# A two-layer graph network with sorted row look-ups on one core: where a group's bias add and count comparison stand, and how many steps the woven streams are counted at

## The chip, the core and the metric

The kernel runs on one core of a Trainium2 chip. A core has a matrix engine (PE, with its weight loads shown as PEld), three engines for elementwise work (VectorE = DVE, ScalarE = ACT, GpSimd = POOL), a queue processor that issues most transfers (SyncE = SP), and 16 DMA engines. Each engine works through its own instruction queue in order and waits on semaphores for the others. The metric is the device time of one execution in microseconds, lower is better; the time of a kernel is the median of its runs.

## What is computed

Inputs are `x` (32 batches of 512 nodes with 256 features) and `adj` (32 x 512 x 512, zeros and ones). Two layers follow one another, each a graph operator and then a feed-forward block, with layer norms and residual sums. The change is in the first layer; its two parts, cut to what matters:

```python
def _L0_gnn_ref(x, adj, W_msg, W_upd, bias):
    a = adj.astype(x.dtype)
    h = jnp.einsum('bnf,fu->bnu', x, W_msg)
    msg_sum = jnp.einsum('bij,biu->bju', a, h)
    deg = jnp.sum(a, axis=1)
    messages = jnp.where(deg[..., None] > 0, msg_sum / jnp.maximum(deg, 1.0)[..., None], 0.0)
    return jax.nn.relu(jnp.einsum('bnf,fu->bnu', x, W_upd) + messages + bias)

def _L0_ffn_ref(x, Wt, bt, sl_cvx, of_cvx, sl_ccv, of_ccv, alpha, Wc, bc, Wg, bg, Wd, bd):
    s = jax.nn.sigmoid(alpha)
    t = jnp.max(xx[:, None, :] + Wt[None, :, :], axis=-1) + bt
    z = t[:, :, None]
    cvx = jnp.max(z * sl_cvx[None] + of_cvx[None], axis=-1)
    ccv = jnp.min(z * sl_ccv[None] + of_ccv[None], axis=-1)
    trop = s * cvx + (1.0 - s) * ccv
    classical = jax.nn.gelu(xf @ Wc + bc, approximate=False)
    g = jax.nn.sigmoid(xf @ Wg + bg)
    return (g * trop + (1.0 - g) * classical) @ Wd + bd
```

The second layer (graph attention with a softmax over typed edges, then a mixer over slices) is built by code that the change does not touch.

## The kernel before

**The maximum by look-ups.** `t` is, for each row of x, a maximum over 256 features of "value of the feature + that feature's row of the table `Wt`". The kernel does not form all 256 sums. For a row it takes the largest values in order, gathers the table rows that belong to them (a table in DRAM, 256 rows of 1024), and keeps a running maximum; after as many look-ups as are needed, smaller values cannot win. How many a row needs is counted for each row ahead of time (the column COUNT of its stored row). Rows are then sorted by that count, so that one tile of 128 rows holds rows of like need. `CAPS` gives the number of look-ups of the 32 tiles of a segment: 24, 9, 7, 6, 5, 5, 5, five times 4, four times 3, seven times 2, nine times 1. A flag `over` records for each row whether its count is above its tile's cap.

**Segments, tiles, groups.** The 32 batches make 4 segments of 8 batches (32 tiles of 128 rows). The feed-forward works on groups of 4 tiles: group g of a segment has the tiles g, g + 8, g + 16, g + 24, so g = 0 holds the tile with 24 look-ups ("heavy") and the others have few ("light"). The order of the 32 groups is (0,7), (0,0) to (0,6), (1,0) to (1,7) and so on.

**Three streams.** All are Python generators; every `yield` ends a step.

- `convs(s)`, one batch after the other: `conv_in` loads x and adj, normalizes (`layer_norm_T`: xna L56, its transposes lnpa L60, copies x1T L62) and multiplies by W_msg (ph L395, copied to h L397); `conv_out` multiplies by W_upd (pu L413, bias sum u L416), sums messages (pm L422, deg and u L425 to L427), normalizes the result (xnb L444), finds the eight largest values and their places (L448, L449), counts (rest L452), and stores the rows (`rows_of`, L458). `put_in_order` sorts a segment's rows.
- `features(raw)`, once at the start: it rearranges the feed-forward's features. A loop of six rounds (L283 to L303) of vector operations turns the slopes and offsets into bends; a key for each feature is stored and read back by all partitions (L328, L330); eight passes (L335) count how many keys are larger, one per block of 128 features; eight scatters (L339) put the features in order in DRAM; from there they are loaded (L348 to L350, L368), transposed (`turn`, L360, L361) and the table is stored (L365).
- `feed_forwards`: for each group `sums`, `mixed` and `down`.
  - `sums(s, g)` gathers the rows of the four tiles (xs L541), asks for the table rows of their largest value (best L552) and goes through the tiles: normalized rows xn (ACT, L562), their transposes into two PSUM tiles xsp (PE, L565), the bias of the output added to the residual in xs (POOL, L566), for caps above 8 more of the largest values (DVE), the comparison for `over` (DVE, L580), the value added to the first table row (ACT, L583), and then for each further look-up a gather of rows (POOL, L586) and a running maximum (DVE, L589, 128 x 1024). It yields after every fourth look-up and after every tile. At the end two copies turn xsp into xnT (ACT, L596).
  - `mixed(s, g)` goes through eight feature blocks f: cls and gate matmuls (PE, L609; ACT, L611), four transposes tz of the maxima (PE, L616), bends (ACT L618, L622; DVE L623), the mixture (DVE, L625 to L627). One step is one f, after a first one.
  - `down(s, g)` multiplies by W_d (po, L638), adds to the residual in xs (DVE, L640) and stores (L641).

**What sets the order.** `woven(a, na, b, nb)` (L68) takes steps of two streams in proportion na to nb. In the first phase convolutions of segment 0 run woven with `features` at 80 to 56. Later `feed_forwards` is woven with the rest of the convolutions and then with layer 1, which follows them. Within a group, `mixed` of the group is woven with `sums` of the next one at 9 to 8. That is the order of recording; a list scheduler of the tile framework then sets the order of each engine's queue by priorities and readiness, and inserts the semaphores. Tile pools bound how far the streams may overlap: a tile whose buffer is still read waits. Those that matter here: PSUM tags with two buffers each, "tp" (the two xsp of `sums`, the pair of a layer norm in `convs`, the transposes in `features`), "mm" (ph, pu, pm, po) and "mf" (cls, gate); in SBUF `best` with seven buffers (four to a group), `rows` with four, `xs` with three, `past` with three.

Of the kernel before, what the change touches and what calls it, by code (L numbers as in the profile page):

```python
# [10 lines left out]
BF16 = mybir.dt.bfloat16  # L11
U32 = mybir.dt.uint32
AF = mybir.ActivationFunctionType
ALU = mybir.AluOpType
# [4 lines left out]
P = 128  # L19
N = 512  # L20
D = 256
NT = N // P
# [74 lines left out]
def layer0_sorted(tc, ident, eps, x, adj, w, x2s, ranks, over, following):  # L97
# [6 lines left out]
    nc = tc.nc  # L104
    B = x.shape[0]
    SEG = B // len(x2s)
    ST = SEG * NT
# [3 lines left out]
    CAPS = [24, 9, 7, 6, 5, 5, 5] + 5 * [4] + 4 * [3] + 7 * [2] + 9 * [1]  # L111
# [3 lines left out]
    NG = ST // NT  # L115

    MEAN, COUNT, VAL, IDX, RW = D, D + 2, D + 3, D + 11, D + 19
# [9 lines left out]
    with ExitStack() as ctx:  # L127
        cst = ctx.enter_context(tc.tile_pool(name="c0", bufs=1))
# [24 lines left out]
        ones = cst.tile([P, 1], BF16, tag="ones0", name="ones0")  # L153
        nc.gpsimd.memset(ones, 1.0)

        count_to = cst.tile([P, P], I32, tag="count_to", name="count_to")
        nc.gpsimd.iota(count_to, pattern=[[1, P]], base=0, channel_multiplier=0)
        upto = cst.tile([P, P], BF16, tag="upto", name="upto")
# [49 lines left out]
        def features(raw):  # L208
# [52 lines left out]
            def pick(key, best):  # L261

                got = []
                for v in (sl, of):
                    other = part("other", four)
                    nc.vector.tensor_tensor(other, key, each(best), ALU.not_equal)
                    key = part("key", four)
                    nc.vector.scalar_tensor_tensor(key, other, -1e30, v, ALU.mult, ALU.add)
                    best = part("got", [P, FC, 2], bufs=4)
                    nc.vector.tensor_reduce(best, key, AX.X, ALU.max)  # L270
                    got.append(best)
                return got
# [11 lines left out]
            for s in range(NS + 1):  # L284
                d, t, out = part("d", four), part("t", four), part("out", four)
                nc.vector.tensor_sub(d, sl, each(slope))
                nc.vector.tensor_sub(t, of, each(offset))
                nc.vector.tensor_scalar(out, d, 0.0, None, ALU.is_le)
                nc.vector.tensor_scalar_max(d, d, 1e-30)
                nc.vector.reciprocal(d, d)  # L290
                nc.vector.tensor_mul(t, t, d)

                nc.vector.scalar_tensor_tensor(t, out, -1e30, t, ALU.mult, ALU.add)
                at = part("at", [P, FC, 2])
                nc.vector.tensor_reduce(at, t, AX.X, ALU.max)
                hit = hits[:, :, s, :]
                nc.vector.tensor_scalar(hit, at, -HI, None, ALU.is_gt)
                if s:
                    nc.vector.tensor_mul(hit, hit, hits[:, :, s - 1, :])
                steeper, offset = pick(t, at)  # L300
                nc.vector.tensor_sub(bend[:, :, s, :, 0], steeper, slope)
                nc.vector.tensor_copy(bend[:, :, s, :, 1], at)
                slope = steeper  # L303
                yield
# [28 lines left out]
            for c in range(FC):  # L333
                more = rtile("more", [P, FFN])
                nc.vector.tensor_scalar(more, every, place[:, 1, c : c + 1], 0.0, ALU.is_gt, ALU.add,  # L335
                                        accum_out=place[:, 2, c : c + 1])
            nc.vector.tensor_copy(number, place[:, 2, :])
            for c in range(FC):
                nc.gpsimd.indirect_dma_start(  # L339
# [191 lines left out]
        def feed_forwards():  # L531


            def sums(s, g):

                tiles = range(g, ST, NG)
                while s not in placed_segs:
                    next(ahead)
                xg = sb.tile([P, NT, RW], F32, tag="xs", name=f"xs{s}_{g}", bufs=3)
                for t, tile_no in enumerate(tiles):  # L540
                    nc.gpsimd.indirect_dma_start(  # L541
                        out=xg[:, t, :], out_offset=None, in_=rows_of[s],
                        in_offset=bass.IndirectOffsetOnAxis(
                            ap=order[:, s * ST + tile_no : s * ST + tile_no + 1].bitcast(U32), axis=0))
                xnT = sb.tile([P, DC, N], F32, tag="xnT", name=f"xnT{s}_{g}")
                pt = [ps.tile([P, NT, P], F32, tag="tp", name=f"xsp{s}_{g}_{c}") for c in range(DC)]
                best = []

                def ask(t):

                    best.append(sb.tile([P, FFN], F32, tag="best", name=f"best{s}_{g}_{t}", bufs=2 * NT - 1))
                    nc.gpsimd.indirect_dma_start(  # L552
                        out=best[t], out_offset=None, in_=table,
                        in_offset=bass.IndirectOffsetOnAxis(ap=xg[:, t, IDX : IDX + 1].bitcast(U32), axis=0))

                ask(0)
                for t, tile_no in enumerate(tiles):
                    if t + 1 < NT - 1:
                        ask(t + 1)
                    r, cap = xg[:, t, :], CAPS[tile_no]  # L560
                    xn = sb.tile([P, D], F32, tag="xn", name=f"xn{s}_{g}_{t}", bufs=2)
                    nc.scalar.activation(xn, r[:, :D], AF.Identity, bias=r[:, MEAN : MEAN + 1],  # L562
                                         scale=r[:, MEAN + 1 : MEAN + 2])
                    for c in range(DC):
                        nc.tensor.transpose(pt[c][:, t, :], xn[:, c * P : (c + 1) * P], ident)  # L565
                    nc.gpsimd.tensor_add(r[:, :D], r[:, :D], bd)  # L566
                    vals, idxs = r[:, VAL : VAL + 8], r[:, IDX : IDX + 8]
                    if cap > 8:
                        rounds = -(-cap // 8)
                        tops = sb.tile([P, 2, 8 * rounds], F32, tag=f"tops{rounds}", name=f"tops{s}_{g}_{t}", bufs=1)  # L570
                        vals, idxs = tops[:, 0, :], tops[:, 1, :]
                        for i in range(rounds):
                            eight = slice(8 * i, 8 * i + 8)
                            nc.vector.max(vals[:, eight], xn)
                            nc.vector.max_index(idxs[:, eight].bitcast(U32), vals[:, eight], xn)
                            if i + 1 < rounds:
                                less = sb.tile([P, D], F32, tag="xn", name=f"less{s}_{g}_{t}_{i}", bufs=2)
                                nc.vector.match_replace(less, vals[:, eight], xn, -3e38)
                                xn = less
                    nc.vector.tensor_scalar(over[:, s * ST + tile_no : s * ST + tile_no + 1],  # L580
                                            r[:, COUNT : COUNT + 1], 2.0 * cap + 1.0 - D, None, ALU.is_gt)
                    m = best[t]
                    nc.scalar.activation(m, m, AF.Identity, bias=vals[:, 0:1])  # L583
                    for k in range(1, cap):
                        row = sb.tile([P, FFN], F32, tag="rows", name=f"rows{s}_{g}_{t}_{k}", bufs=4)
                        nc.gpsimd.indirect_dma_start(  # L586
                            out=row, out_offset=None, in_=table,
                            in_offset=bass.IndirectOffsetOnAxis(ap=idxs[:, k : k + 1].bitcast(U32), axis=0))
                        nc.vector.scalar_tensor_tensor(m, row, vals[:, k : k + 1], m, ALU.add, ALU.max)  # L589
                        if k % 4 == 3:  # L590
                            yield
                    if t == NT - 2:
                        ask(NT - 1)
                    yield
                for c in range(DC):
                    nc.scalar.copy(xnT[:, c, :], pt[c].rearrange("p t n -> p (t n)"))  # L596
                got[s, g] = xg, xnT, best

            def mixed(s, g):
# [45 lines left out]
            groups = [(0, NG - 1)]  # L645
            groups += [(s, g) for s in range(len(x2s)) for g in range(NG) if (s, g) != groups[0]]
            yield from sums(*groups[0])
            for i, now in enumerate(groups):
                steps_ = mixed(*now)
                next(steps_)  # L650
                if i:
                    down(*groups[i - 1])
                yield
                more = sums(*groups[i + 1]) if i + 1 < len(groups) else iter(())
                yield from woven(steps_, 9, more, 8)
            down(*groups[-1])

        def all_convs():
# [10 lines left out]
        with tc.tile_pool(name="r0", bufs=1) as raw:  # L669
            first = iter(lambda: next(ahead), 0)  # L670
            next(first)
            bounds(raw)
            for _ in woven(first, SEG * 10, features(raw), 56):
                pass
        sb = ctx.enter_context(tc.tile_pool(name="s0", bufs=2, reuse_waits="tile"))

# [1547 lines left out]
```

## Time and profile before

| what | value |
|---|---|
| median of 3 runs | 4619.16 us (4616.48 to 4621.86) |
| the profiled execution, its own time | 4623.49 us |
| its span | 4621.6 us |
| mean granted PE clock | 0.951 |
| PE busy | 4067.9 us, 88% |
| DVE, ACT, POOL busy | 73%, 50%, 37% |
| first cls matmul of the feed-forward | at 324 us |
| last batch's rows of the convolutions stored | at 1906 us |
| layer 1 alone | from about 2500 us |

In the profile times are microseconds from the start of the span; Lnnn is a line of the kernel before. A line of the waits reads: engine, tile and line that waited, the engine, tile and line that ended the wait, total, times, longest. A line of the timeline reads: start, duration, engine, line, operation, tile written <- tiles read, shapes, number, and in brackets how long the engine was idle before it and what released it. In the rows of the costliest groups the number before the bar is a count, then busy time and mean nanoseconds of one, then the idle time ahead of it. Some matmul records are missing from the trace, so counts of matmuls in a short stretch can be too low.

### The profile page before, as it was taken

How to read it: one execution, taken by the hardware profiler on the slowest of the kernel's cores; microseconds unless marked ns; L12 is line 12 of the kernel's file. 1: busy time of each engine (PE TensorE's matmuls, PEld its weight loads, DVE VectorE, ACT ScalarE, POOL GpSimd, SP SyncE). 2: the span in 40 equal slices, each digit the busy share in tenths (PEclk: the TensorE clock that was granted, in tenths of full speed). 3: DMA queues.
4: the chain of work that ended last, by engine and by line, in shares of the span. 5: the costliest groups of instructions: out<-in, count | busy, mean ns of one | idle time of the engine just before them, and what ended most of it. 6: DMA issues, size and time to landing. Idle time of an engine off the chain costs nothing. (4 is left out here: it accounts for less than half of the span.)

```text
span 4621.6 us, 56127 instructions
## 1 busy us (share of the span) xinstructions
PE 4067.9 (88%) x19287; PEld 2525.4 (55%) x19287; DVE 3379.1 (73%) x7040; ACT 2291.7 (50%) x4756; POOL 1729.5 (37%) x2027
## 2 busy tenths in 40 slices
PE   5768898988988889888897899999999999999987
PEld 4545655656556566555554355555555555555555
DVE  6678778887788877777775777777787777777763
ACT  2344555545655556555564444545544454454432
POOL 2356444653435534353332223222323323332220
PEclk8889999999999999998998999999999999999998
DMA  5556433653436533374431111111111111111100
GB/s 125 172 158 214 164 127 126 198 178 124 136 118 198 177 129 112 99 263 145 141 115 48 53 46 56 51 48 44 44 54 49 56 56 53 47 54 56 40 14 15
DMA packets 235100, 474.09 MB, mean 103 GB/s; under 512 B 38299, under 2 KB 114075, under 8 KB 234804
## 3 DMA queue, kind: packets, MB, share of 16 engines
q0 software_dynamic: 80256, 282.38, 19.3%
q1 hardware_dynamic: 154548, 188.02, 13.3%
q8 instruction: 154, 2.52, 0.2%
q14 instruction: 142, 1.16, 0.1%
HBM read 413.16 MB, written 57.16 MB: 102 GB/s over the span
## 5 line engine op out<-in xcount | busy, mean ns | idle before, releaser
L609 PE MATMUL clsp<-xnT,wc 128*128 128x512 f32 x1024 | 512.1, 621 | 77.3 <-ACT cls L611 63.0
L609 PE MATMUL gatep<-xnT,wg 128*128 128x512 f32 x1024 | 497.7, 605 | 16.0 <-ACT gate L611 13.2
L638 PE MATMUL po<-wd,acc 128*128 128x256 f32 x2048 | 450.9, 381 | 0.4 <-DVE acc L627 0.3
L638 PEld LDWEIGHTS po<-wd,acc 128*128 128x128 f32 x2048 | 391.4, 191 | 65.9 <-issue 13.8
L422 PE MATMUL pm<-h,adj 128*128 128x257 f32 x1024 | 295.5, 435 | 136.3 <-DVE xs L640 67.3
L589 DVE SCALAR_TENSOR_TENSOR best<-rows,xs,best 128x1024 f32<-128x1024 f32 x212 | 276.1, 1305 | 165.4 <-ACT best L583 98.1
L623 DVE SCALAR_TENSOR_TENSOR acc<-past,fld,acc 128x512 f32<-128x512 f32 x448 | 351.1, 787 | 54.3 <-ACT past L622 45.5
L1198 DVE SCALAR_TENSOR_TENSOR att<-own,other,mask 128x512 f32<-128x512 f32 x512 | 378.9, 762 | 11.5 <-DMA own<-ownd 11.0
L586 POOL DMA_INDIRECT rows<-table,xs x212 | 261.1, 1232 | 237.3 <-DVE best L589 171.8
L609 PEld LDWEIGHTS gatep<-xnT,wg 128*128 128x128 f32 x1024 | 195.8, 195 | 260.5 <-issue 197.0
L622 ACT ACTIVATE past<-tz,fld 128x512 f32<-128x512 f32 x448 | 291.0, 694 | 83.4 <-DVE acc L623 83.0
L618 ACT ACTIVATE acc<-tz,fld 128x512 f32<-128x512 f32 x256 | 199.5, 779 | 265.1 <-PE tz L616 262.0
L422 PEld LDWEIGHTS pm<-h,adj 128*128 128x128 f32 x1024 | 212.4, 218 | 194.5 <-issue 106.7
L1231 PE MATMUL avp<-att,hv 128*64 128x512 f32 x1024 | 310.3, 628 | 4.2 <-DVE att L1198 4.2
L609 PEld LDWEIGHTS clsp<-xnT,wc 128*128 128x128 f32 x1024 | 185.7, 197 | 222.3 <-issue 121.1
L1331 PE MATMUL yTp<-sw,x 128*128 128x512 f32 x512 | 242.7, 614 | 39.8 <-DVE sw L1326 32.3
L611 ACT ACTIVATE cls<-clsp,fld 128x512 f32<-128x512 f32 x256 | 176.7, 690 | 201.7 <-PE clsp L609 86.9
L1319 PE MATMUL lgp<-wsl,x4T 128*128 128x512 f32 x512 | 252.0, 628 | 27.9 <-DVE mask L1070 21.7
L1139 POOL DMA_INDIRECT x<-x2s,ranks x128 | 140.9, 1101 | 343.0 <-DVE att L1198 104.1
L1284 POOL TENSOR_TENSOR mu<-mu,eps 128x16 f32<-128x16 f32 x32 | 121.3, 3791 | 324.2 <-DVE mu L1283 323.1
L611 ACT ACTIVATE gate<-gatep,fld 128x512 f32<-128x512 f32 x256 | 175.6, 686 | 127.5 <-PE gatep L609 103.6
L541 POOL DMA_INDIRECT xs<-rows_of,order x128 | 143.4, 1121 | 250.7 <-DVE acc L623 78.7
(597 smaller groups left out, 8961.5 us busy)
## 6 DMA issues: line engine op xcount, KB each, us to landing
adji<-in_adj SPq DMA_DIRECT2D x128, 256.0 KB
ai<-in_adj SPq DMA_DIRECT2D x128, 256.0 KB
own<-ownd SPq DMA_DIRECT2D x128, 256.0 KB
rows_of<-keep SPq DMA_DIRECT2D x32, 550.0 KB
x<-in_x SPq DMA_DIRECT2D x32, 512.0 KB
x2s<-xs SPq DMA_DIRECT2D x32, 512.0 KB
out<-x SPq DMA_DIRECT2D x32, 512.0 KB
rows<-table,xs POOLq DMA_INDIRECT x212
```

The lines of the kernel that those rows point to most:

```text
L422: nc.tensor.matmul(pm[:, : D + 1], a[:, i, t * P : (t + 1) * P], h[:, i, :], start=i == 0, stop=i == NT - 1)
L586: nc.gpsimd.indirect_dma_start(out=row, out_offset=None, in_=table, in_offset=bass.IndirectOffsetOnAxis(ap=idxs[:, k : k + 1].bitcast(U32) ...
L589: nc.vector.scalar_tensor_tensor(m, row, vals[:, k : k + 1], m, ALU.add, ALU.max)
L609: nc.tensor.matmul(pf, wf[:, c, f * P : (f + 1) * P], xnT[:, c, :], start=c == 0, stop=c == DC - 1)
L611: nc.scalar.activation(o, pf, fn, bias=fld[:, f, bf : bf + 1], scale=1.0 if fn == AF.Gelu else 0.5)
L622: nc.scalar.activation(r, z, AF.Relu, bias=fld[:, f, AT + b : AT + b + 1])
L623: nc.vector.scalar_tensor_tensor(y, r, fld[:, f, CH + b : CH + b + 1], y, ALU.mult, ALU.add)
L638: nc.tensor.matmul(po[:, i, :], acc[f][:, t * P : (t + 1) * P], wd[:, f, :], start=f == 0, stop=f == FC - 1)
L1198: nc.vector.scalar_tensor_tensor(e, own[h], other[:, j, h : h + 1], mask[:, j, :], ALU.max, ALU.mult)
L1231: nc.tensor.matmul(pv[q][k * HO : (k + 1) * HO, :], hv[:, j, h, :HO], weighed[b, h, j], start=j == 0, stop=j == NT - 1)
L1319: nc.tensor.matmul(pf, xnT[:, c, t * P : (t + 1) * P], wsl[:, c, :], start=c == 0, stop=c == DC - 1)
L1331: nc.tensor.matmul(py, xn[:, t, c * P : (c + 1) * P], sw[:, t, :], start=t == 0, stop=t == NT - 1)
```

## The change

It has three parts.

1. In `features`, three places yield more: two in each of the six rounds and one after each of the eight counting passes (20 more steps); the count at which `features` is woven goes from 56 to 74.
2. In `sums`, the bias add and the comparison leave the loop over tiles and stand at the end of the group: one comparison over the four tiles against a constant tile `limits` of 128 x 32, which nine memsets on POOL fill at the start, and four bias adds.
3. `mixed` and the next `sums` are woven at 9 to the number of steps that these sums have, one for each tile and one for each four look-ups: 11 for g = 0, then 7, 6, 6, 5, 5, 5, 5 for g = 1 to 7, in place of 8 always.

```diff
+        limits = cst.tile([P, ST], BF16, tag="limits", name="limits")
+        for i, cap in enumerate(CAPS):
+            if i == 0 or cap != CAPS[i - 1]:
+                nc.gpsimd.memset(limits[:, i:], 2.0 * cap + 1.0 - D)
...
                 nc.vector.tensor_scalar_max(d, d, 1e-30)
+                yield
                 nc.vector.reciprocal(d, d)
...
                     nc.vector.tensor_mul(hit, hit, hits[:, :, s - 1, :])
+                yield
                 steeper, offset = pick(t, at)
...
                 nc.vector.tensor_scalar(more, every, place[:, 1, c : c + 1], 0.0, ALU.is_gt, ALU.add,
                                         accum_out=place[:, 2, c : c + 1])
+                yield
...
-                    nc.gpsimd.tensor_add(r[:, :D], r[:, :D], bd)
...
-                    nc.vector.tensor_scalar(over[:, s * ST + tile_no : s * ST + tile_no + 1],
-                                            r[:, COUNT : COUNT + 1], 2.0 * cap + 1.0 - D, None, ALU.is_gt)
...
                 for c in range(DC):
                     nc.scalar.copy(xnT[:, c, :], pt[c].rearrange("p t n -> p (t n)"))
+                nc.vector.tensor_tensor(over[:, s * ST : (s + 1) * ST].rearrange("p (t g) -> p g t", g=NG)[:, g, :],
+                                        xg[:, :, COUNT], limits.rearrange("p (t g) -> p g t", g=NG)[:, g, :],
+                                        ALU.is_gt)
+                for t in range(NT):
+                    nc.gpsimd.tensor_add(xg[:, t, :D], xg[:, t, :D], bd)
...
-                yield from woven(steps_, 9, more, 8)
+                steps = sum(1 + CAPS[n] // 4 for n in range(groups[(i + 1) % len(groups)][1], ST, NG))
+                yield from woven(steps_, 9, more, steps)
...
-            for _ in woven(first, SEG * 10, features(raw), 56):
+            for _ in woven(first, SEG * 10, features(raw), 74):
```

## The prediction

> **What bounds the kernel now.** First the page's busy times, then busy time by stretch: start of the layer, feed-forward with the next convolutions woven in, feed-forward alone, layer 1. Columns of the second: stretch, length, busy us (instructions) of PE, PEld, DVE, ACT, POOL, granted clock, DMA share, GB/s.
>
> ```profile
> PE 4067.9 (88%) x19287; PEld 2525.4 (55%) x19287; DVE 3379.1 (73%) x7040; ACT 2291.7 (50%) x4756; POOL 1729.5 (37%) x2027
> ...
> 0.00:324.00 324.00, 207.04 (x874) 161.93 (x875) 209.34 (x764) 111.87 (x238) 118.03 (x316) 0.84 0.50 147
> 324.00:2057.00 1733.00, 1523.45 (x5760) 1000.95 (x5759) 1355.75 (x2669) 943.56 (x1617) 862.46 (x1131) 0.96 0.49 157
> 2057.00:2500.00 443.00, 400.61 (x1419) 243.79 (x1418) 313.24 (x439) 254.19 (x402) 150.87 (x137) 0.95 0.38 122
> 2500.00:4621.00 2121.00, 1936.85 (x11240) 1118.74 (x11238) 1500.76 (x3171) 982.05 (x2501) 598.15 (x444) 0.97 0.16 47
> ```
>
> PE is the bound. Layer 1 (from 2500) keeps its order, so the change can only touch PE's idle time before it: 324 − 207 = 117 us, 1733 − 1523 = 210 us, 443 − 401 = 42 us. Next the waits of 324 to 2500 (total us, times, longest), to see what that idle time is:
>
> ```profile
> PE pm L422 <- DVE xs L640: 67.3, 16, 8.0
> PE clsp L609 <- ACT cls L611: 63.0, 41, 6.3
> ...
> PE ph L395 <- DVE xs L640: 16.0, 2, 8.6
> ```
>
> ```profile
> DVE best L589 <- ACT best L583: 110.7, 21, 7.4
> ...
> DVE over L580 <- DMA xs<-rows_of,order: 46.1, 45, 6.7
> ```
>
> ```profile
> POOL xs L566 <- ACT xn L562: 207.0, 51, 14.6
> ```
>
> The two named parts wait visibly: the comparison (L580) 46.1 us on DVE, the bias add (L566) 207.0 us on POOL. PE's largest waits, 67.3 + 16.0 = 83.3 us in 18 waits, are for the residual add (L640), at boundaries between groups. One of them in the timeline (start, duration, instruction, idle before it):
>
> ```profile
> 1054.34 0.60 PE L616 MATMUL tz<-ident,best 128*128 128x128 f32 x4
> ...
> 1056.06 1.03 POOL L552 DMA_INDIRECT best<-table,xs  x1 [0.16 <-issue]
> ...
> 1063.37 1.15 ACT L583 ACTIVATE best<-best,xs 128x1024 f32<-128x1024 f32 x1 [4.92 <-DMA best<-table,xs]
> ...
> 1066.16 5.25 DVE L589 SCALAR_TENSOR_TENSOR best<-rows,xs,best 128x1024 f32<-128x1024 f32 x4 [6.60 <-ACT best L583]
> ...
> 1081.24 0.68 DVE L640 TENSOR_TENSOR xs<-xs,po 128x512 f32<-128x512 f32 x1
> ...
> 1082.07 2.48 PE L422 MATMUL pm<-h,adj 128*128 128x257 f32 x5 [7.76 <-DVE xs L640]
> ```
>
> The chain: the last transpose (1054.34) frees `best`; its gather lands; ACT adds the value (1063.37); DVE's row maxima start (1066.16, 11.8 us after the transpose) and the second residual add stands behind them on DVE; PE waits 7.76 us. Steps or no steps, these sums cannot start before that transpose.
>
> **The change part by part.** All prices are against the profiled run, 4623.5 us (span 4621.6); the median shown is 4619.2, 4.3 lower. The built queues give the new order.
>
> *Comparison and bias.* DVE loses 128 comparisons of 147 ns and gains 32 wider ones, at about the old row's longest, 155 ns: 18.8 − 5.0 = 13.9 us of busy time, credited at 0 since DVE is 78% busy (1355.75/1733) where PE waits for chains. The scheduler does not leave the comparison at the end: in the built order it stands where the gathers land, one wait in place of four. It matters where an overdue comparison holds DVE, in the last groups, with no convolution beside them:
>
> ```profile
> 2319.82 0.15 DVE L580 TENSOR_SCALAR over<-xs 128x1 f32<-128x1 f32 x1 [1.39 <-DMA xs<-rows_of,order]
> ...
> 2320.66 0.69 ACT L611 ACTIVATE gate<-gatep,fld 128x512 f32<-128x512 f32 x1 [2.35 <-DVE acc L626]
> ...
> 2321.40 1.99 PE L609 MATMUL clsp<-xnT,wc 128*128 128x512 f32 x4 [2.29 <-ACT gate L611]
> ```
>
> Two comparisons waited 1.16 + 1.39 there, behind them stood the mixing's L626, for which ACT's gate waited, and PE lost 2.29 behind that. Five such groups at about half of it: −6. Bounds: −11.5 if all of it is gained; +6 if the one comparison waits for the fourth gather with L626 still behind it, as long again as half of the two did (2.55/2 × 5). The 128 adds of 747 ns stay on POOL, queued near their tile, so POOL's 207 us stay too; behind them stand gathers for the next tile, and only 8.2 us of PE waited on an add: 0 (±8).
>
> The nine memsets (98 ns each by L152: 0.9 us) lie in POOL's 8.85 us wait at 3 to 12 us: 0; without that cover, 0.9.
>
> [...]
>
> *Step counts.* 9 against 8 becomes 9 against 11 for sums of g = 0, then 7, 6, 6, 5, 5, 5, 5. Fewer steps mean that the next group's sums are recorded faster through the mixing. At seven light boundaries the built order holds the two "tp" buffers for the sums until the mixing ends, so that the convolution's layer norm comes later, into the boundary: 8 lnpa transposes (2 × 0.60) and 16 ph (3.78), 5.0 us of PE. The ACT work goes with it, ahead of the value adds: two xnT (0.59 each), xn 0.60, xna 0.59, four xnb (0.59), two x1T (0.59), four rest (0.51), two h (0.57): 9.1 us. ACT idled 4.92 at this place (the row at 1063.37), so 4.2 to 4.5 us stick out, and the row maxima start that much later; PE has 5.0 us more to do meanwhile. Net about −0.5 each, called 0. Bounds: all 9.1 us in the way, +4.1 × 7 = +29; none, −5.0 × 7 = −35.
>
> Before heavy mixings (g = 0; after groups 6 and 14) some 16 us of convolution matmuls now stand ahead of `po`, and there
>
> ```profile
> 852.04 3.78 PE L395 MATMUL ph<-w_msg,x1T 128*128 128x256 f32 x8 [7.44 <-DVE xs L640]
> ```
>
> had a twin of 8.57. Both waits go, −16.0; eight row maxima more stand in those gaps, 8 × 1.28 = 10.2, of which I take half as exposed: −11. Bounds −16 to +10 (waits stay, all eight exposed).
>
> *Features in shorter steps.* 20 more yields against 18 more in the count. Counted in steps, the chain ends at 73.5 of some 100 convolution steps (68 × 80/74; before 48 × 80/56 = 68.6): 4.9 steps, at 12 a batch of about 20 us, 8 us later. SP's queue says more: there the store of `keys`, the loads of `sorted_rows` and the store of `table` each stand behind one more batch's `rows_of`, so about 20 us later. The last copies of the chain run at 212 now; at 232 they still lie ahead of the first gather from `table` (275) and the first cls (324), so the cover, 275 − 212 = 63 us, holds; with it gone the delay would be paid in full, +8 to +20. Stage one's DVE work only changes places between batches. Five comparisons in a row, with 7.6 us of waiting at 268 to 276, stand ahead of a convolution's bias sum; one wait is left of them. I take −2 (−10 to +10, as batches before or after get the DVE first).
>
> SP's other changes are loads of x that pass a load of adj or a store of x2s at a few boundaries; SP waits for nothing new, and each issue took about 0.38 us (L379, L641): 0.
>
> Sum: −6 + 0 + 0 − 11 − 2 = −19, of which I take off 5 for new waits that such a reordering leaves elsewhere (PE's 63.0 us on cls L611 are the next in line): −14. 4623.5 − 14 = 4609.5; on the median's footing 4605.
>
> **Rivals.**
> *Slower: ACT in the way.* Place: the seven light boundaries, ACT's queue ahead of the value add L583. If most of the 9.1 us is new delay, each costs +4.1: +29, the heavy −11 fails too, −6 − 2 + 5 stay: about +26, 4645. It decides once the row maxima start 7.5 us or more later than 11.8 after the last transpose (2.5 × 7 = 18 cancels the gains). For it: PE waits 83 us at just these boundaries already. Against it: ACT's 4.92 us idle and 50% load.
>
> *Nothing.* The scheduler puts comparison and adds back where their data land, and the features' chain has its cover; the boundaries cancel: 4619 ± 5. For it: the built order does the first; against it, that nine boundaries do change.
>
> *Far faster.* The 5.0 us moved in costs no delay, as PE waits 7.76 there: −35 − 11 − 6 − 2 + 5 = −49, 4570. For it: ACT's idle time; against it: the row maxima wait for ACT (110.7 us).
>
> **How the numbers follow.** Forecast 0.42, ACT in the way 0.27, nothing 0.16, far faster 0.15. A measurement tells 0.2% (9.2 us) from no change. The forecast's own spread (4590 to 4617) is beyond that line three times in four; so faster 0.42 × 0.75 + 0.15 = 0.47, same 0.10 + 0.15 = 0.25, slower 0.28. The range 4572 to 4646 leaves out half of the far faster case and half of the slower one: 0.2.
>
> **What would show it.** Right: row maxima about 16 us after the last transpose at light boundaries, PE's wait for L640 down from 83 to about 65 us, the two heavy waits gone, comparisons' wait below 35 us, POOL's wait for xn still near 200, the features' last copies near 232 and the first cls still at 316 to 326, layer 1 as long as before (2121). Wrong: row maxima 19 us or more after it and L640's waits above 100 us; first cls past 330, which would mean that the features' chain or its convolutions lost their cover; or a new wait of over 20 us in the feed-forward that no row above names.

## The result, and the profile after

| | before | after |
|---|---|---|
| median of 8 runs | 4622.19 us (4607.51 to 4635.2) | 4602.43 us (4594.19 to 4612.24) |
| ratio to before | | 0.9967, 95% interval 0.9947 to 0.9986 |
| span of the profiled execution | 4621.6 us | 4610.5 us |
| first cls matmul | 324.0 | 327.0 |
| first matmul of layer 1 behind the feed-forward | 2514.6 | 2507.4 |

The change makes the kernel faster by 0.33% (0.14 to 0.53%), 15 us by the ratio; the prediction said 4605 us. The ratio, made of runs side by side on a chip, is what counts: the medians of before alone wandered between 4614 and 4622 from one set of runs to the next. The profiled execution after took 4612.2 us, 10 more than its kernel's median.

The same view by stretch as ahead of the prediction (stretch, length, busy us and instructions of PE, PEld, DVE, ACT, POOL, granted clock, DMA share, GB/s), for the kernel after:

```profile
0.00:324.00 324.00, 204.08 (x859) 158.99 (x860) 206.73 (x751) 109.53 (x234) 113.12 (x321) 0.85 0.50 147
324.00:2057.00 1733.00, 1545.08 (x5796) 1007.99 (x5794) 1356.65 (x2619) 948.52 (x1624) 880.13 (x1140) 0.95 0.49 158
2057.00:2500.00 443.00, 400.42 (x1418) 241.71 (x1416) 306.48 (x413) 252.32 (x399) 144.51 (x133) 0.95 0.37 118
2500.00:4611.00 2111.00, 1929.39 (x11218) 1110.23 (x11218) 1498.45 (x3163) 981.76 (x2501) 596.13 (x443) 0.97 0.16 47
```

In the second stretch PE is busy 21.6 us longer (1545.1 against 1523.5), that is, idle by as much less; the start is idle 3 us longer and the last groups of the feed-forward as long as before. Where the idle time went shows in PE's waits of 324 to 2500:

```profile
PE clsp L619 <- ACT cls L621: 56.4, 36, 7.4
PE pm L430 <- DVE xs L650: 40.4, 14, 6.0
PE pm L430 <- DVE u L435: 37.4, 12, 6.4
PE clsp L619 <- ACT gate L621: 18.7, 15, 5.9
...
PE ph L403 <- DVE xs L650: 8.7, 2, 4.4
```

and, of the kernel before, three that are needed here and below:

```profile
PE pm L422 <- DVE u L427: 20.2, 9, 6.2
...
PE lnpa L60 <- ACT xna L56: 8.3, 4, 5.3
PE pm L422 <- DVE u L416: 7.8, 6, 2.2
```

The residual add's waits (L640 before, L650 now) fell from 67.3 to 40.4, and those of ph from 16.0 to 8.7: from 83.3 to 49.1 us in all. Another wait rose: that of the message matmul pm for u (L427 before, L435 now), from 20.2 to 37.4. DVE and POOL, the two that the change names:

```profile
DVE over L602 <- DMA xs<-rows_of,order: 55.0, 16, 8.4
```

```profile
POOL xs L606 <- ACT xn L570: 189.6, 34, 17.9
```

A third of the waits, but not less waiting: 55.0 us in 16 against 46.1 in 45 for the comparison, 189.6 against 207.0 for the bias add.

The boundary between groups (1,1) and (1,2), the same one as ahead of the prediction, in the timeline of the kernel after:

```profile
1047.30 0.60 PE L626 MATMUL tz<-ident,best 128*128 128x128 f32 x4
...
1053.11 3.77 PE L403 MATMUL ph<-w_msg,x1T 128*128 128x256 f32 x16
...
1058.21 1.15 ACT L588 ACTIVATE best<-best,xs 128x1024 f32<-128x1024 f32 x1
...
1063.05 2.60 DVE L594 SCALAR_TENSOR_TENSOR best<-rows,xs,best 128x1024 f32<-128x1024 f32 x2 [4.58 <-ACT best L588]
...
1075.19 0.68 DVE L650 TENSOR_TENSOR xs<-xs,po 128x512 f32<-128x512 f32 x1
1075.82 1.28 DVE L594 SCALAR_TENSOR_TENSOR best<-rows,xs,best 128x1024 f32<-128x1024 f32 x1
...
1076.02 1.98 PE L430 MATMUL pm<-h,adj 128*128 128x257 f32 x8 [2.74 <-DVE xs L650]
...
1077.62 1.27 DVE L594 SCALAR_TENSOR_TENSOR best<-rows,xs,best 128x1024 f32<-128x1024 f32 x1
```

The last of DVE's row maxima in the kernel before, ahead of its second residual add at 1081.24:

```profile
1077.12 1.28 DVE L589 SCALAR_TENSOR_TENSOR best<-rows,xs,best 128x1024 f32<-128x1024 f32 x1 [0.41 <-DMA rows<-table,xs]
1078.77 2.54 DVE L589 SCALAR_TENSOR_TENSOR best<-rows,xs,best 128x1024 f32<-128x1024 f32 x2 [0.37 <-DMA rows<-table,xs]
```

The convolution's ph (3.77 us) stands in the boundary now, and lnpa beside it. The value add runs 10.9 us after the group's last transposes (1058.21 − 1047.30; before 9.0) and the row maxima start 15.7 us after them (before 11.8), 3.9 us later. But the second residual add comes only 1.0 us later than before (27.9 after the transposes against 26.9): two of the nine row maxima, at 1075.82 and 1077.62, now stand behind it, where all nine stood ahead, and 2 × 1.28 = 2.6 us is most of the difference. PE waits 2.74 us in place of 7.76. That is 5 us of work put into a wait that grew by 1.0.

The same matmuls stand in six boundaries now, after (0,1), (0,2), (1,0), (1,1), (2,0) and (2,1). PE's idle time from the last transposes to the message matmul that waits for the second residual add, summed from the timeline, was 7.8, 4.1, 7.6, 7.8, 7.8 and 8.0 us and is 3.2, 3.2, 5.0, 3.3, 3.6 and 3.3, 21.5 us less. The second of them is a check of the reading: after (0,2) no row maximum moved behind the second residual add, and there the add is as late as the row maxima (4.1 and 3.8 us later than before) and PE gains only 0.9 us.

### The profile page after: what moved, and what is told of

The parts are those of the page before. It is cut to its first block, busy times and chain, and to the rows that moved or that the text cites. A ratio compares the mean times of both kernels' runs of the same rounds, so it can differ in the third digit from the quotient of the medians.

```text
span 4610.5 us, 56109 instructions
## 1 busy us (share of the span) xinstructions
PE 4079.0 (88%) x19287; PEld 2518.9 (55%) x19287; DVE 3368.3 (73%) x6944; ACT 2292.1 (50%) x4756; POOL 1733.9 (38%) x2036
## 3 DMA queue, kind: packets, MB, share of 16 engines
q14 instruction: 141, 1.16, 0.1%
## 5 line engine op out<-in xcount | busy, mean ns | idle before, releaser
L619 PE MATMUL clsp<-xnT,wc 128*128 128x512 f32 x1024 | 526.6, 633 | 76.5 <-ACT cls L621 56.4
L591 POOL DMA_INDIRECT rows<-table,xs x212 | 253.0, 1193 | 215.7 <-DVE best L594 160.3
L619 PEld LDWEIGHTS clsp<-xnT,wc 128*128 128x128 f32 x1024 | 188.3, 201 | 226.4 <-issue 121.3
L621 ACT ACTIVATE cls<-clsp,fld 128x512 f32<-128x512 f32 x256 | 175.1, 684 | 208.6 <-PE clsp L619 102.3
L1342 PE MATMUL yTp<-sw,x 128*128 128x512 f32 x512 | 243.7, 617 | 36.4 <-DVE sw L1337 29.0
```

What stands on the lines that cost most here:

```text
L591: nc.gpsimd.indirect_dma_start(out=row, out_offset=None, in_=table, in_offset=bass.IndirectOffsetOnAxis(ap=idxs[:, k : k + 1].bitcast(U32) ...
L619: nc.tensor.matmul(pf, wf[:, c, f * P : (f + 1) * P], xnT[:, c, :], start=c == 0, stop=c == DC - 1)
L621: nc.scalar.activation(o, pf, fn, bias=fld[:, f, bf : bf + 1], scale=1.0 if fn == AF.Gelu else 0.5)
L1342: nc.tensor.matmul(py, xn[:, t, c * P : (c + 1) * P], sw[:, t, :], start=t == 0, stop=t == NT - 1)
```

## The experiments

All ratios are to the kernel before, from runs on the same chip, with their 95% intervals. "Stage" is the stretch from the first cls matmul to the first matmul of layer 1, and idle its length less PE's busy time, both from the view by stretch: 2190.6 − 1928.6 = 262.0 us before, 2180.4 − 1942.6 = 237.8 after.

**1. The step counts alone.**

```diff
-                yield from woven(steps_, 9, more, 8)
+                steps = sum(1 + CAPS[n] // 4 for n in range(groups[(i + 1) % len(groups)][1], ST, NG))
+                yield from woven(steps_, 9, more, steps)
```

> Before with nothing changed but the step count at which the next group's sums are woven (11 for g = 0, then 7, 6, 6, 5, 5, 5, 5 instead of 8). Theory (the order around the heavy mixings makes the gain): nearly the whole gain of the change is here, -10 to -20 us against before (ratio 0.996 to 0.998), PE's wait for the residual add (L640) in 324 to 2500 down from 83 to about 50 us, and the mixing of g = 7 with its heavy sums 10 to 25 us longer but that of g = 0 about 15 shorter. Rival (the comparison and bias at the end make it): within 4 us of before, L640's waits still near 83.

Measured: 4604.32 us, ratio 0.9971 (0.9961 to 0.9982), −13 us; stage idle 241.0; the residual add's waits 45.3 + 8.5 us. The gain of the change is here.

**2. Comparison and bias at the end, alone**: the parts of the change in `sums` with `limits`, 8 steps, features as before.

> Before with only the comparison and the bias adds at the end of a group's sums (and the nine memsets). Theory: within 5 us of before (ratio 0.999 to 1.001): DVE has some 10 us less to do but is not the bound, and the one comparison waits for the last of four gathers, so its waits are not below before's 46 us. Rival: -8 us or more, with L640's waits down by 30 us.

Measured: 4609.65 us, ratio 0.9977 (0.9966 to 0.9989), −11 us, more than the theory allows; stage idle 256.7 (5 less than before), first cls 3 us sooner (320.6), the comparison's wait 56.9 us in 18, the residual add's waits 54.1 + 16.0. Neither side has it: the rival's time, but not its mark (the waits down by 30 us; they fell by 13).

**3. The features' shorter steps alone**: the three yields and the count 74.

> Before with only the 20 more yields in the features' chain and the count 74. Theory: the first cls matmul, which came at 324 in before and at 327 in the change, comes at 324 to 330 and the time is within 5 us of before (ratio 0.9995 to 1.001): the cover of 63 us holds. Rival 1 (the shorter steps help the convolutions): first cls at 316 or sooner and -6 us. Rival 2 (the chain's cover is gone): first cls past 335 and +10 us.

Measured: 4620.92 us, ratio 1.0006 (0.9991 to 1.002), first cls at 325.9, stage idle 261.3. No gain, and nothing lost that this can tell; the first theory stands.

**4. The change without the features' part.**

> The changed kernel with the features' chain as before (no added yields, count 56). Theory: as the change or a few us faster, -12 to -20 us against before (ratio 0.9957 to 0.9975), first cls back at 324. Rival (the features' steps carry part of the gain): only -5 us or less.

Measured: 4607.35 us, ratio 0.9977 (0.9967 to 0.9988), −11 us; stage idle 243.7. Slightly less than forecast, but beside 0.9971 for the steps alone and 0.9967 for the whole the intervals overlap. What follows: the ends add nothing that shows on top of the steps, though alone they showed −11 us. It is not that both move the same convolution work into the boundaries: in the profile of run 2 ph still stands ahead of the last transposes after (1,1), and PE's idle time at that boundary is within half a microsecond of the kernel before. Why the ends help alone stays open.

**5. and 6. The step counts taken apart**: 11 for the heavy sums alone, and the light groups' counts alone.

```diff
-                yield from woven(steps_, 9, more, 8)
+                steps = 11 if groups[(i + 1) % len(groups)][1] == 0 else 8
+                yield from woven(steps_, 9, more, steps)
```

> Before with the step count 11 only where the next group is g = 0, else 8 as before. Steps alone gave -13.4 us (ratio 0.9971). Theory (both places share it): the pairs of groups around the heavy mixings of segments 0 to 2 lose 3 to 7 us each, none where the convolutions are done (group (3,0)), in all -5 to -10 us against before; PE's idle time within 20 us after a light boundary as in before (7.8 us at the boundaries after groups (0,1), (1,1), (2,1)). Forecast as it was made: -11. Rival (light boundaries make it all): within 3 us of before.

```diff
                 steps = sum(1 + CAPS[n] // 4 for n in range(groups[(i + 1) % len(groups)][1], ST, NG))
+                if groups[(i + 1) % len(groups)][1] == 0:
+                    steps = 8
                 yield from woven(steps_, 9, more, steps)
```

> Before with the step count of each light group's sums (7, 6, 6, 5, 5, 5, 5) and 8 as before for g = 0. Theory: PE's idle time after the boundaries behind (0,1), (1,1), (2,1) falls from 7.8 to about 3.3 us, as in steps alone, since 5 us of convolution matmuls lie there and the row maxima start only 1 to 2 us later; a part comes back as waits of the message matmuls for u (L427), 20 us in before; -4 to -9 us against before. The forecast had about 0 here. Rival (ACT in the way): +5 us or more, row maxima 16 us or more after the last transpose.

Measured: heavy 4609.18 us, ratio 0.9998 (0.9987 to 1.0008); light 4592.33 us, ratio 0.9961 (0.9948 to 0.9974). The rival of the first has it: the light groups make the whole gain, −18 us, twice what the theory of the second gave them, and the 11 steps nothing that the time shows. Stage idle was 253.8 in the heavy run and 241.6 in the light one. The wait of ph for the residual add, heavy and light:

```profile
PE ph L395 <- DVE xs L640: 15.0, 2, 7.7
```

```profile
PE ph L395 <- DVE xs L640: 9.0, 2, 4.7
```

It was 16.0 before: the light counts shorten it, the 11 steps hardly. The same boundary as above in the run with the light counts, in the timeline:

```profile
1033.21 3.77 PE L395 MATMUL ph<-w_msg,x1T 128*128 128x256 f32 x16
...
1056.51 2.90 PE L422 MATMUL pm<-h,adj 128*128 128x257 f32 x8 [3.13 <-DVE xs L640]
```

ph is in the boundary and PE's wait is 3.13 us; the idle time at the six boundaries is 22.5 us below that of the kernel before (3.5, 3.0, 3.4, 3.7, 3.5, 3.5). The row maxima are as late as in the change, 15.7 us after the last transposes at (1,1), close to the 16 or more that the rival had named; its loss is not there. PE's waits of 324 to 2500 by name:

```profile
PE clsp L609 <- ACT cls L611: 50.2, 34, 7.3
PE pm L422 <- DVE u L427: 39.6, 12, 6.2
PE pm L422 <- DVE xs L640: 34.8, 15, 4.6
```

The residual add's wait is lower still than in the change (34.8 against 40.4), and u is as high (39.6 against 20.2 before): some of the gain comes back one step later. That DVE, with row maxima still to do, is then late for the next message matmuls is the likely reason; no run takes it apart.

**7. The comparison in the last stage of the group**: the change, with the comparison taken out of `sums` and put into `down`, once a group, behind its two residual adds (not twice, as the expectation has it).

> The changed kernel with the comparison moved once more, from the end of the group's sums into the last stage of the group (after each residual add, so twice a group). Theory: DVE's 55 us of waiting for the gathers at the comparison goes to under 10, but DVE is not the bound there, so within 5 us of the changed kernel (ratio against before 0.996 to 0.998). Rival (the comparison's wait holds the mixing's DVE work and through ACT the PE): -8 us or more against the changed kernel, PE's wait of clsp for ACT (56 us) down by 15 us.

Measured: 4600.67 us, ratio 0.9972 (0.9963 to 0.9982): no different from the change. But its wait did not go: 55.7 us in 16, the same, and in the last groups it waits 2.7 to 2.8 us each time for the same gathers as in the change. The scheduler put the comparison back where its data land, so this run can't tell what that wait costs; that stays open.

**8. The down projection copied out of PSUM by ACT**, on top of the change.

```diff
-                    nc.vector.tensor_add(xg[:, t0 : t0 + 2, :D], xg[:, t0 : t0 + 2, :D], po)
+                    pc = sb.tile([P, N], F32, tag="past", name=f"poc{s}_{g}_{t0}", bufs=3).rearrange("p (t d) -> p t d", t=2)
+                    nc.scalar.copy(pc, po)
+                    nc.vector.tensor_add(xg[:, t0 : t0 + 2, :D], xg[:, t0 : t0 + 2, :D], pc)
```

> The changed kernel with the down projection copied out of PSUM by ACT, into a buffer of the bends (past), and the residual add reading the copy: ACT has 64 copies of about 0.6 us more, 38 us, and DVE's adds no longer hold the two mm buffers. Theory (what is left at the boundaries is that the second residual add stands behind the row maxima on DVE): PE's waits for the residual add, 40.4 + 8.7 us in the changed kernel, are gone, and the time falls by 15 to 35 us against it (ratio against before 0.989 to 0.994). Rival (the next thing, DVE's u, ends the wait at the same time): the same wait shows up as pm waiting for u, and the time is within 5 us of the changed kernel. Rival 2: the copies stand ahead of the value adds on ACT and cost 5 us or more.

Measured: 4570.04 us, ratio 0.9905 (0.989 to 0.992), −44 us against before and some 29 against the change; stage idle 225.4. No wait for the residual add is left, and the theory has the time. It doesn't have all of the account: stage idle fell by only 12.4 where 49.1 us of waits went, since cls (56.4 to 68.8), u (37.4 to 46.8) and lnpa (6.5 to 15.4) are waited for longer and ph waits 7.6 us for the copy. Part of what rival 1 named is there. The other 24.1 us by which this profile's stage is shorter are shorter matmuls; the last section comes back to these.

**9. and 10. The copy with the light counts, without and with the ends.**

> Before with the light groups' step counts (8 kept for g = 0) and the down projection copied out of PSUM by ACT; neither the features' steps nor the ends. Theory (the two gains lie at the same boundaries, but one fills PE's wait and the other removes it, so they overlap): light steps gave -18 us, the copy -30 us on top of the change; together -40 to -52 us against before (ratio 0.989 to 0.9915), and a few us faster than the changed kernel with the copy (0.9905) since the 11 steps of g = 0 cost 3 to 6 us a heavy group. Rival (the copy alone does it, the step counts then have nothing to fill): as the changed kernel with the copy or slower, 0.9905 to 0.993.

> As the run before (light steps, copy by ACT) with the comparison and bias at the end of the sums added. Theory (the ends only take some waits from DVE that is not the bound): within 5 us of it. Rival (the ends are worth the -10 us they showed alone): 8 us or more faster than it.

Measured: 4575.34 us, ratio 0.9907 (0.9891 to 0.9923), and 4569.67 us, ratio 0.9901 (0.9884 to 0.9917). Runs 8, 9 and 10 can't be told apart: the step for g = 0 and the ends make no difference that shows, as the theory of the second had it, and the few us that the theory of the first promised are not seen. Run 9's ratio lies within its rival's bounds too; that the copy alone does not do it is for run 12 to show. Any of the three is faster than both kernels; the last by 46 us against before.

**11. Five steps for every group, the heavy ones too.**

```diff
-                yield from woven(steps_, 9, more, 8)
+                yield from woven(steps_, 9, more, 5)
```

> Before with 5 in place of 8 for every group, the heavy ones too: that is what half of the light groups got, and 6 less than the change gives g = 0. Theory (what pays is that the next group's sums of a light group are recorded to their end inside the mixing; for heavy sums fewer steps leave more of the look-ups behind the mixing): -10 to -22 us against before (ratio 0.995 to 0.998), the three triples of groups around a heavy mixing as with light steps or up to 4 us longer. Rival (the heavy groups need their steps): each triple 6 us or more longer than in before and the whole within 3 us of it.

Measured: 4592.23 us, ratio 0.9957 (0.9942 to 0.9971), −20 us; stage idle 226.4. A constant does as well as the count by look-ups, and heavy sums with 5 steps lose nothing that the time shows: the number must be small for the light groups, and that is all that these runs show of it.

**12. The copy by ACT alone**, on the kernel before.

> Before with only the down projection copied out of PSUM by ACT; steps 8, no other part of the change. Theory (the change's gain is that convolution matmuls fill PE's wait for the residual add; take that wait away and there is nothing left to fill): PE's waits for the residual add, 83 us in before, are gone, and the time is near that of the copy with the step counts (0.9901 to 0.9907): -34 to -46 us against before (ratio 0.990 to 0.9927). Rival (the step counts pay by themselves): -15 to -30 us (ratio 0.9935 to 0.9967), so that the steps still add 14 us or more on top.

Measured: 4599.91 us, ratio 0.9965 (0.995 to 0.998), −16 us: the theory is wrong and the rival's time is met. PE's waits, 324 to 2500:

```profile
PE clsp L609 <- ACT cls L611: 94.2, 45, 8.8
PE pm L422 <- DVE u L427: 45.2, 12, 9.4
PE lnpa L60 <- ACT xna L56: 19.2, 7, 5.4
PE pm L422 <- DVE u L416: 15.7, 8, 3.1
```

The 83.3 us for the residual add are gone, as they should be, but clsp's wait rose by 31 (63.0 to 94.2), u's by 33 (20.2 + 7.8 to 45.2 + 15.7), lnpa's by 11: 75 of the 83 come back under other names, and stage idle fell by only 15.6 (to 246.4). Freed from one buffer, PE ran ahead and stopped at the next thing in its queue. With the light counts as well (run 9), which put convolution work there, stage idle is 227.9, and the two together give 0.9907, where apart they gave 0.9961 and 0.9965.

## Why the prediction was right, and where its sum was not

The time, the direction and the size are right (4605 forecast, 4602 measured), and what was said of the bound is right: what was gained is idle time of PE before layer 1. The terms of the sum are not right: errors of both signs cancel, so that the total came out as forecast is luck.

- *Light boundaries, "Net about −0.5 each, called 0"*: wrong. Run 6 gives −18 us (−12 to −24). The 5.0 us of PE work did move in, and the row maxima do start 3.9 us later at (1,1), where 4.2 to 4.5 were forecast and "about 16 us after the last transpose" was the mark (15.7). The step that failed is the next one: that delay was carried over whole to the second residual add, which PE waits for, as if everything ahead of it on DVE stayed ahead of it (as it does after (0,2) alone). In the new queue two row maxima of 1.28 us have moved behind it there and after (2,1), one at three of the other places, and it came 1.0 us later. So some 5.0 − 1.0 = 4.0 is gained at such a place (21.5 over the six, 3.6 each), near what the rival "far faster" took (5.0); that rival's total was too high, as the heavy part and the last groups gave nothing that shows and the wait of pm for u rose. PE's waits for the residual add fell to 49.1, where 65 was the mark.
- *Heavy mixings, "−11"*: wrong. Run 5 gives −1 us (−6 to +4), though its stage idle is 8 us lower. The waits that it was read from did halve in the whole change (16.0 to 8.7), but run 6, without the 11 steps, has 9.0 as well: the light counts of the groups next to them do it.
- *Last groups, "−6"*: not seen; PE is idle 42.6 us from 2057 to 2500, where it was 42.4. The one comparison waits as long as the two did, for the last gather; here at the place of the prediction's line at 2319.82:

```profile
2313.34 0.62 DVE L602 TENSOR_TENSOR over<-xs,limits 128x4 f32<-128x4 f32 x1 [2.76 <-DMA xs<-rows_of,order]
```

  2.76 us here against 1.16 + 1.39 before. That is the wait which the pessimistic end of the term's bounds went by; its loss of 6 us is not seen either. The forecast said that the comparison's waits would fall below 35 us; they rose to 55.0.
- *Bias adds, 0*: right in kind: POOL's wait for xn stayed near 200 (189.6), and PE waited no more than 2 us for these adds. The new place of the adds did not lengthen DVE's row maxima: those of 324 to 2500 took 428 us in all, where they took 431, and the add's longest is 1.9 us now, where it was 3.6.
- *Ends as a whole, near −6*: −11 alone (run 2), nothing that shows on top of the steps (run 4). Why they help alone is not settled.
- *Features, "−2"*: +3 us (−4 to +9) in run 3, inside its bounds. The delay was read wrong: the copies at the chain's end were expected near 232 and end at 215.7, against 212.7 before. The first gather of rows comes 3.4 us later (271.95 against 268.59) and the first cls 3.0, at 327.0, just past the 316 to 326 of the forecast.
- *The 5 us held back for new waits*: there was such a wait, larger and at another place: the message matmuls' wait for u rose by 17 us (20.2 to 37.4), that for cls, the one named, fell (63.0 to 56.4).

The rival "ACT in the way" has the place and the lateness (15.7 us, below the 19 from which it decides), but run 6 refutes its price; "nothing" is refuted by the ratio's interval.

## What to carry to other kernels

A delay at the head of a chain (3.9 us at (1,1)) is not the delay at its end (1.0 us there): follow the new queue down to the instruction that the bounding engine waits for, and count what now stands behind it. A wait at a buffer was worth here what the engine could do in its place: filling it with work that was needed anyway paid almost in full (22.5 us less idle time at the six boundaries, 20.4 in the stage), while with the buffer freed early alone 75 of 83 us came back under other names, and the two together paid no less than their sum (43 us, 36 to 50; 18 and 16 apart). And a total that comes out right proves no term of its sum; the two halves of one line of the change, run apart, showed the opposite shares of those forecast.

## What the runs showed of the hardware that was not expected

PE's busy time for the same instructions was not a constant. In the stage of the feed-forward it was 1928.6 us before, 1942.6 after, and 1915.3 with the light counts. The kernel before and after over that stage, by the view by stretch:

```profile
324.00:2514.60 2190.60, 1928.64 (x7197) 1248.44 (x7195) 1673.44 (x3124) 1198.37 (x2020) 1021.00 (x1277) 0.95 0.47 149
```

```profile
327.00:2507.40 2180.40, 1942.59 (x7196) 1247.35 (x7195) 1662.27 (x3033) 1198.58 (x2019) 1028.69 (x1277) 0.95 0.47 150
```

Idle time fell by 24.2 us, but the matmuls took 14.0 longer, so that the stage is 10.2 shorter. The clock records of the trace say how: the clock was granted at half in stretches of 3.41 us (22 in the stage before, 21 after), 6.83 (14 and 17), 10.24 (1 and 2), 17.07 (1 and 2) and 20.48 (1 and 0), the last in time of each profile running past the stage's end, in all for 207.6 us of the stage before, 231.2 after and 175.1 with the light counts. What sets these stretches off no run shows. Matmuls were longer in them: in the kernel before one of clsp (128x512) took 593 ns at full clock and 1062 at half, one of pm (128x257) 381 and 636 (medians). Over thirteen profiles of this case (all but that of run 7) PE's busy time in the stage rises by 0.50 us for each microsecond at half clock (correlation 0.89).

Each profile is one execution, but the mean granted clock of the other runs is on record, of before those beside the experiments, and by it the 14 us belong to these two executions rather than to the change. Within one kernel the time falls by about 2.4 us for each 0.001 of clock (193 runs, correlation −0.63). Between kernels the mean clock hardly differs: 0.9519 for the kernel after (8 runs) and 0.9517 with the step counts alone (12), against 0.9519 before (35 runs, those beside run 1); with the light counts 0.9532 (6) against 0.9529 (23). Run 8 has 0.9546, with an error of 0.0012 from 5 runs, so that a few of its 44 us may be the clock's. The clock is a reason why a gain read off one profile's idle time (24 us) and the ratio of the medians (15 us) differ, and why executions of one kernel lay 28 us apart.
